# A graph network's last 96 nodes updated in three sets of 32 across the partitions' quarters, and the last messages' mish in three parts

## The chip, the cores and the metric

The kernel runs on one core of a Trainium2 chip. The metric is the device time of one execution in microseconds (us); the time of a version is the median of its runs. Engines are called TensorE (PE in the profile), VectorE (DVE), ScalarE (ACT), GpSimd (POOL) and SyncE (SP, which here only issues DMAs).

## The reference

625 nodes with 512 features and 20,000 edges sorted by their target pass through four graph layers, each behind a layer norm, a relu and a residual. The change touches only the fourth. In it, per edge and then per node:

```
def mish(x):
    return x * jnp.tanh(jax.nn.softplus(x))
edge_feat = jnp.concatenate([x[src], x[dst], edge_attr], axis=-1)
h = mish(edge_feat @ W1 + b1)
messages = mish(h @ W2 + b2)
agg = jax.ops.segment_sum(messages, dst, num_segments=x.shape[0])
u = mish(jnp.concatenate([x, agg], axis=-1) @ W3 + b3)
out = u @ W4 + b4
y = x + out
return (y - mu) * jax.lax.rsqrt(var + LN_EPS) * gamma + beta
```

## The kernel before

The fourth layer is `layer3_near`. Edges come in 160 tiles of 125, four to a group, 40 groups (NG = 40, g = 0 to 39). A hand-written loop over steps s = 0 to 44 is a software pipeline: in step s group s gets its first product, group s-2 its second, group s-4 is summed into its targets, and group s-5's sums are added to the nodes' sums. The stages are:

- `rows` (two steps ahead): edge features by SP, gathered node rows by POOL.
- `first(g)`: TensorE makes z for 500 edges (L1327, L1332), DVE adds the bias (L1334) and writes a copy bounded at 20 (`bounded`, L1291). `quotients` then lets ACT compute the factor of the mish in place, exp (L1299), ln(1 + .) (L1301), tanh (L1303), and DVE multiplies it in (L1477). Exp then ln then tanh need two loads of ACT's function tables; `set_of_exp` (L1307) loads the table that holds exp and ln ahead of need.
- `second(g)`: four tiles of 16 products, each evicted by DVE with its bias (L1348) to the messages; one step later they are bounded into `um`, go through ACT, and in the step after that are multiplied (L1468). The last group has parts of its own: its messages are bounded in two halves (tiles 0-1 and 2-3) as soon as they are there, ACT does exp and ln of each half and then both tanh (L1490 to L1493), and `sent` multiplies by halves (L1361).
- `sent(g)`: TensorE sums messages to a window of 32 nodes through a one-hot (L1370), with the 512 features in four quarters of the partitions; DVE copies the sum (L1374).
- `collected(g)`: a transpose (L1380), and DVE adds it into mT, the nodes' sums (L1381).

The nodes are updated in five sets of 125 (c = 0 to 4), each when the last group that reaches into it has been collected: `last_of` is 8, 16, 24, 32 and 39. With last group L, `update_u` (products with W3, L1391; add, L1394; bounded copy, L1291) is in step L+5, ACT's three functions in L+6, `update_mul` (L1399) and `update_turn` (four transposes, L1405; copy to uT, L1407) in L+7, `update_out` (products with W4, L1422; add, L1424; statistics, L1425, L1426) in L+8, and `update_root`, `update_end` (square root on ACT, L1431; normalization, L1435 to L1441; store, L1443) in L+9. Set 4 has no steps left: its whole chain, and the root and end of set 3, stand behind the loop. Set 4's output is made in two halves of 256 columns.

What sets the order: everything wrapped in `keep` stays in program order on its engine, so DVE and ACT work through the loop body as written, in order. TensorE's instructions are placed by the scheduler, and are also executed in the order that it gives. A tile from a pool takes one of `bufs` buffers of its tag. Whoever writes a buffer anew waits until the last reader of the tile before it is done. PSUM tiles of `ps` have six buffers. The node updates use tags with one buffer each:

```
u = lp.tile([128, D], F32, tag="u", name="u", bufs=1)[:P]
us["u", c] = bounded(u, P, D, "uu", 1)
uT = lp.tile([128, D], F32, tag="uu", name="uT", bufs=1)[:, :KD * P]
```

So the bounded copy of a set and the transposed u of a set share the one buffer `uu`.

Of the kernel before, what the change touches and what calls it, by code (L numbers as in the profile page):

```python
# [9 lines left out]
F32 = mybir.dt.float32  # L10
F16 = mybir.dt.float16
I32 = mybir.dt.int32
AF = mybir.ActivationFunctionType
# [181 lines left out]
def gnn_body(ctx: ExitStack, tc: tile.TileContext, a: dict, out: bass.AP, consts, near: bool):  # L195
# [1028 lines left out]
    def layer3_near(wts, wm2, own, h_tabs, uh):  # L1224

        keep = tc.keep_in_program_order
        with tc.tile_pool(name="layer3n", bufs=2) as lp, banks("c", 6):
# [65 lines left out]

            width = {"uz": G * D}

            def quotients(v):

                for u in v:
                    keep(nc.scalar.activation(u, u, AF.Exp))  # L1299
                for u in v:  # L1300
                    keep(nc.scalar.activation(u, u, AF.Ln, bias=1.0))  # L1301
                for u in v:
                    keep(nc.scalar.activation(u, u, AF.Tanh))  # L1303
# [34 lines left out]
            def second(g):  # L1338

                z = zs.pop(g)  # L1340
                w = G // z.shape[1]
                m = lp.tile([P, G, D], F32, tag="mess", name="mess", bufs=3)
                for j in range(G):
                    p = ps("z2")
                    for f in range(KD):
                        nc.tensor.matmul(p[:P, :], z[:, j // w, f, j % w * P:(j % w + 1) * P], wm2[:, f, :],  # L1346
                                         start=f == 0, stop=f == KD - 1)
                    keep(nc.vector.tensor_add(m[:, j, :], p[:P, :], bc["b2"]))  # L1348
                    if g == NG - 1 and j % 2:

                        us["m", g, j // 2] = bounded(flat(m[:, j - 1:j + 1, :]), P, 2 * D, "uz", 2)
                ms[g] = m

            def sent(g):


                m = ms.pop(g)
                if g == NG - 1:
                    for n in range(2):
                        v = flat(m[:, 2 * n:2 * n + 2, :])  # L1360
                        keep(nc.vector.tensor_mul(v, v, us.pop(("m", g, n))))  # L1361
                base = base_of(g)
                acc[g] = pools["acc"].tile([128, 128], F32, tag="acc", name="agg3", bufs=2)
                o = work.tile([P, G, W], F32, tag="oh", name="oh")
                nc.vector.tensor_tensor(o, iota_f[:, None, base:base + W].to_broadcast([P, G, W]),
                                        dst_f[:, g * G:(g + 1) * G, None].to_broadcast([P, G, W]),
                                        op=ALU.is_equal)
                for j in range(G):
                    for i in range(KD):
                        nc.tensor.matmul(acc[g][i * W:(i + 1) * W, :], o[:, j, :],  # L1370
                                         m[:, j, i * 128:(i + 1) * 128], start=j == 0, stop=j == G - 1,
                                         skip_group_check=True, tile_position=(0, i * W))
                v = lp.tile([128, 128], F32, tag="ag", name="ag", bufs=2)
                keep(nc.vector.tensor_copy(v, acc[g]))  # L1374
                acc[g] = v
# [7 lines left out]
                                          mT[:, :, base:base + W]))  # L1383


            last_of = [max(g for g in range(NG) if base_of(g) < (c + 1) * P) for c in range(NC)]

            def update_u(c):
                p = ps("u")
                for k in range(KD):  # L1390
                    nc.tensor.matmul(p[:P, :], mT[:, k, c * P:(c + 1) * P], late["w"][:, k, :],  # L1391
                                     start=k == 0, stop=k == KD - 1)
                u = lp.tile([128, D], F32, tag="u", name="u", bufs=1)[:P]
                keep(nc.vector.tensor_add(u, p[:P, :], uh[:, c, :]))  # L1394
                nodes[c] = u
                us["u", c] = bounded(u, P, D, "uu", 1)

            def update_mul(c):
                keep(nc.vector.tensor_mul(nodes[c], nodes[c], us.pop(("u", c))))  # L1399

            def update_turn(c):
                u = nodes.pop(c)
                t = ps("tr")
                for k in range(KD):
                    nc.tensor.transpose(t[:, k * P:(k + 1) * P], u[:, k * 128:(k + 1) * 128], ident[:P, :P])  # L1405
                uT = lp.tile([128, D], F32, tag="uu", name="uT", bufs=1)[:, :KD * P]
                keep(nc.vector.tensor_copy(uT, t[:, :KD * P]))  # L1407
                nodes[c] = uT

            def update_out(c):  # L1410
                uT = nodes.pop(c)
                y = h[:, c, :]

                n = 2 if c == NC - 1 else 1
                stats = work.tile([P, 2, 6], F32, tag="stats3", name="stats3", bufs=NC)[:, :n]
                mv = work.tile([P, 2], F32, tag="mv1", name="mv1", bufs=NC)
                rstd = work.tile([P, 1], F32, tag="rstd1", name="rstd1", bufs=NC)
                for i in range(n):
                    cols = slice(i * D // n, (i + 1) * D // n)
                    p = ps("o3")  # L1420
                    for k in range(KD):
                        nc.tensor.matmul(p[:P, :D // n], uT[:, k * P:(k + 1) * P], late["wm4"][:, k, cols],  # L1422
                                         start=k == 0, stop=k == KD - 1)
                    keep(nc.vector.tensor_add(y[:, cols], p[:P, :D // n], y[:, cols]))  # L1424
                    keep(nc.vector.bn_stats(stats[:, i, :], y[:, cols]))  # L1425
                keep(nc.vector.bn_aggr(mv, stats))  # L1426
                nodes[c] = y, mv, rstd

            def update_root(c):
                y, mv, rstd = nodes[c]  # L1430
                keep(nc.scalar.activation(rstd, mv[:, 1:2], AF.Sqrt, bias=eps))  # L1431

            def update_end(c):
                y, mv, rstd = nodes.pop(c)
                keep(nc.vector.reciprocal(rstd, rstd))  # L1435
                n = 2 if c == NC - 1 else 1
                for i in range(n):
                    cols = slice(i * D // n, (i + 1) * D // n)
                    keep(nc.vector.scalar_tensor_tensor(y[:, cols], y[:, cols], mv[:, 0:1], bc["gamma"][:, cols],
                                                        op0=ALU.subtract, op1=ALU.mult))  # L1440
                    keep(nc.vector.scalar_tensor_tensor(x[:, c, cols], y[:, cols], rstd, x[:, c, cols],  # L1441
                                                        op0=ALU.mult, op1=ALU.add))
                    (nc.scalar if i else nc.sync).dma_start(out[c * P:(c + 1) * P, cols], x[:, c, cols])  # L1443

            def biases(c):
                keep(nc.vector.tensor_add(uh[:, c, :], uh[:, c, :], bc["b3"]))
# [5 lines left out]
            for s in range(NG + 5):  # L1452
# [8 lines left out]
                if s == 0:  # L1461
                    for n in range(2):
                        quotients([us["z", 0, n]])
                        z = flat(zs[0][:, n])
                        keep(nc.vector.tensor_mul(z, z, us.pop(("z", 0, n))))  # L1465
                if s - 4 in ms and s - 4 < NG - 1:
                    m = flat(ms[s - 4])
                    keep(nc.vector.tensor_mul(m, m, us.pop(("m", s - 4))))  # L1468
                if s - 3 in ms and s - 3 < NG - 1:
                    us["m", s - 3] = bounded(flat(ms[s - 3]), P, G * D, "um", 1)  # L1470
                quotients([us[k] for k in (("z", s, 0), ("m", s - 3), *(("u", c) for c in range(NC - 1) if s - 6 == last_of[c])) if k in us])
                for c in range(NC - 2):
                    if s - 9 == last_of[c]:
                        update_root(c)
                if s - 1 in zs and s > 1:
                    z = flat(zs[s - 1][:, 0])
                    keep(nc.vector.tensor_mul(z, z, us.pop(("z", s - 1, 0))))  # L1477
                for c in range(NC - 1):
                    if s - 7 == last_of[c]:
                        update_mul(c)  # L1480
                if s == 1:
# [2 lines left out]
                if 1 <= s - 2 < NG:  # L1484
                    second(s - 2)
                if s - 2 == NG - 1:
                    v = [us["m", NG - 1, n] for n in range(2)]
                    set_of_exp()
                    for u in v:
                        keep(nc.scalar.activation(u, u, AF.Exp))  # L1490
# [1 line left out]
                    for u in v:  # L1492
                        keep(nc.scalar.activation(u, u, AF.Tanh))  # L1493
                    set_of_exp()
                for c in range(NC - 1):
                    if s - 7 == last_of[c]:
                        update_turn(c)
                    if s - 8 == last_of[c]:
# [2 lines left out]
                        update_end(c)  # L1501
                if 9 <= s < 9 + NC:
                    biases(s - 9)
                if 0 <= s - 4 < NG:
                    sent(s - 4)
                if 0 <= s - 5:
                    collected(s - 5)
                for c in range(NC - 1):
                    if s - 5 == last_of[c]:
                        update_u(c)  # L1510
            c = NC - 1
            update_u(c)
            quotients([us["u", c]])
            update_root(c - 1)
            update_mul(c)
            update_turn(c)
            update_end(c - 1)
            update_out(c)
            update_root(c)
            update_end(c)  # L1520

    if near:
        wts2 = ctx.enter_context(tc.tile_pool(name="wts2", bufs=1))
# [87 lines left out]
```

## Time and profile before

| what | value |
|---|---|
| median of 7 runs | 1801.81 us (1798.13 to 1806.59) |
| profiled execution's own time | 1799.09 us |
| its span, first to last instruction | 1797.3 us |
| PE, DVE, ACT, POOL busy | 94%, 56%, 42%, 45% of the span |
| TensorE's mean granted clock | 0.977 of full speed |
| largest line | L1346 (`second`), 556.2 us of PE |

The page counts an engine busy while it executes; an idle time is put down to the instruction whose end released the next one. Late in the kernel a step of the loop takes some 18.7 us (two starts of L1346, 1690.68 and 1709.42). Times below are us from the start of the span.

### The profile page before, as it was taken

How to read it: one execution, taken by the hardware profiler on the slowest of the kernel's cores; microseconds unless marked ns; L12 is line 12 of the kernel's file. 1: busy time of each engine (PE TensorE's matmuls, PEld its weight loads, DVE VectorE, ACT ScalarE, POOL GpSimd, SP SyncE). 2: the span in 40 equal slices, each digit the busy share in tenths (PEclk: the TensorE clock that was granted, in tenths of full speed). 3: DMA queues.
4: the chain of work that ended last, by engine and by line, in shares of the span. 5: the costliest groups of instructions: out<-in, count | busy, mean ns of one | idle time of the engine just before them, and what ended most of it. 6: DMA issues, size and time to landing. Idle time of an engine off the chain costs nothing.

```text
span 1797.3 us, 24375 instructions
## 1 busy us (share of the span) xinstructions
PE 1696.8 (94%) x9770; PEld 876.6 (49%) x9770; DVE 1013.3 (56%) x1697; ACT 761.4 (42%) x792; POOL 811.9 (45%) x479
## 2 busy tenths in 40 slices
PE   4878999999999889999999899999999999999995
PEld 4878544444444334444544444445444444544443
DVE  7997210002000478877854667777666776667663
ACT  2452110000000312222214676766686687668664
POOL 0000000000000377665715888888887788788300
PEclk9999999999999989999999999999999999999996
DMA  2001030020000296756535587666666666667300
GB/s 74 3 3 51 4 133 14 0 94 6 0 0 0 65 203 162 173 153 165 145 88 142 105 175 150 128 117 117 122 127 108 123 129 118 111 115 135 46 1 14
DMA packets 157219, 162.59 MB, mean 90 GB/s; under 512 B 97546, under 2 KB 104059, under 8 KB 157096
## 3 DMA queue, kind: packets, MB, share of 16 engines
q0 software_dynamic: 131584, 119.48, 34.1%
q1 hardware_dynamic: 20100, 32.69, 5.8%
q10 hardware_dynamic: 5412, 8.77, 1.7%
q8 instruction: 79, 1.29, 0.3%
q14 instruction: 44, 0.36, 0.1%
HBM read 155.11 MB, written 5.12 MB: 89 GB/s over the span
## 4 chain that ended last, share of the span: by engine, by line
PE 86%; DVE 4%; issue 3%; DMA 3%; ACT 2%; POOL 1%; DVEq 0%; ACTq 0%; POOLq 0%; SPq 0%
PE z L1346 29%; PE agg L661 10%; PE hb L648 8%; PE sum L961 6%; PE tpw L938 4%; PE q L538 4%; PE z L1332 4%; PE z L1327 4%; PE agg L1370 2%; PE xsd L1040 2%; PE agg L637 2%; PE l L613 2%; PE mlp L890 2%; PE nsum L606 1%; PE u L1391 1%
## 5 line engine op out<-in xcount | busy, mean ns | idle before, releaser
L1346 PE MATMUL z<-wm,z 128*125 128x512 f32 x1280 | 556.2, 592 | 2.7 <-DVE z L1465 2.7
L1346 PEld LDWEIGHTS z<-wm,z 128*125 128x125 f32 x1280 | 237.2, 188 | 293.1 <-issue 269.9
L281 POOL DMA_INDIRECT g_s<-xs,src_i x160 | 296.3, 1852 | 124.2 <-issue 75.7
L281 POOL DMA_INDIRECT g_s<-xd,dst_i x144 | 307.4, 2135 | 43.9 <-issue 42.6
L902 POOL MEMSET mT<- 128x5000 f32 x1 | 4.3, 4265 | 585.8 <-PE tr L843 585.8
L281 POOL DMA_INDIRECT gup<-up,src_i x160 | 199.5, 1247 | 107.2 <-issue 39.7
L1348 DVE TENSOR_TENSOR mess<-z,b 125x512 f32<-125x512 f32 x160 | 106.3, 686 | 134.8 <-PE z L1346 134.8
L661 PE MATMUL agg<-hb,adj 125*125 125x512 f32 x400 | 173.6, 592 | 0.0
L651 DVE COPY hb<-hb 125x512 f32<-125x512 f32 x20 | 13.8, 692 | 263.0 <-PE hb L648 263.0
L945 DVE TENSOR_TENSOR msg<-tpw,gup 125x768 f32<-125x768 f32 x160 | 151.4, 946 | 0.0
L538 PE MATMUL q<-rh,ohs 125*128 125x96 bf16 (+1 forms) x2400 | 120.4, 213 | 28.4 <-DVE ohs L556 26.3
L1334 DVE TENSOR_SCALAR z<-z,b 128x500 f32<-128x500 f32 (+1 forms) x164 | 108.4, 718 | 59.3 <-PE z L1332 57.5
L1299 ACT ACTIVATE uz<-uz 128x2000 f32<-128x2000 f32 (+1 forms) x41 | 75.0, 1829 | 151.3 <-DVE uz L1291 151.3
L648 PE MATMUL hb<-basis,hT 128*125 128x512 f32 x320 | 138.6, 592 | 0.0
L538 PEld LDWEIGHTS <-ohs 125*128 125x128 bf16 x2400 | 115.3, 101 | 33.7 <-DVE ohs L556 32.9
L961 PE MATMUL sum<-msg,ohy 125*32 125x256 f32 (+2 forms) x1600 | 125.8, 392 | 0.0
L653 ACT COPY hb<-hb 125x512 f32<-125x512 f32 x20 | 11.7, 586 | 260.1 <-PE hb L648 240.2
L661 PEld LDWEIGHTS agg<-hb,adj 125*125 125x125 f32 x400 | 74.8, 188 | 94.7 <-issue 94.7
L961 PEld LDWEIGHTS sum<-msg,ohy 125*32 125x32 f32 x1600 | 74.8, 110 | 85.7 <-issue 60.3
L938 PE MATMUL tpw<-w,hid 64*125 64x512 f32 x320 | 99.3, 649 | 6.4 <-DVE msg L945 6.4
L1299 ACT ACTIVATE um<-um 125x2048 f32<-125x2048 f32 x39 | 74.5, 1910 | 71.1 <-DVE um L1291 71.1
L943 DVE TENSOR_TENSOR msg<-tpw,gup 125x256 f32<-125x256 f32 x160 | 66.6, 416 | 59.4 <-PE tpw L938 29.3
(210 smaller groups left out, 2207.4 us busy)
## 6 DMA issues: line engine op xcount, KB each, us to landing
rt<-in_edge_attr SPq DMA_DIRECT2D x76, 125.0 KB
basis<-in_L_gnn_basis SPq DMA_DIRECT2D x8, 1024.0 KB
gup<-up,src_i POOLq DMA_INDIRECT x160
g_s<-xs,src_i POOLq DMA_INDIRECT x160
g_s<-xd,dst_i POOLq DMA_INDIRECT x144
w<-in_L_gnn_W SPq DMA_DIRECT2D x2, 1024.0 KB
loop<-in_L_gnn_loop SPq DMA_DIRECT2D x2, 1024.0 KB
w1ab<-in_L_gnn_W ACTq DMA_DIRECT2D x1, 2048.0 KB
```

The lines of the kernel that those rows point to most:

```text
L281: return nc.gpsimd.indirect_dma_start(out=dst, out_offset=None, in_=table, in_offset=bass.IndirectOffsetOnAxis(ap=idx[:, t:t + 1], axis=0) ...
L538: nc.tensor.matmul(q[c][:, :n, o:o + WT], hot[j][:, c, :], rhs[j][:, q0:q0 + n, :], start=j + k == 0, stop=j == GS - 1 and k == 2, skip_gr ...
L648: nc.tensor.matmul(p[:P, :], hT[:, k, s * P:(s + 1) * P], basis[b][:, k, :], start=k == 0, stop=k == KD - 1)
L661: nc.tensor.matmul(acc[c], adj[:, s - 1, l * NB + b, c * P:(c + 1) * P], hb[:, b, :], start=False, stop=s == NC and b == NB - 1)
L938: nc.tensor.matmul(p[:P, :], hid[s // 2][s % 2][rws, i * P:(i + 1) * P], w4[rws].rearrange("p k u -> p (k u)"), start=True, stop=True)
L945: nc.vector.tensor_mul(m[:, :, 1:, :], pv[:, 2:4, None, :].to_broadcast([P, 2, 3, MUL]), g[:, None, 1:, :].to_broadcast([P, 2, 3, MUL]))
L961: nc.tensor.matmul(A[r * W:(r + 1) * W, cs, :], oh[:, j, q, :], v, start=j % G == 0 and r not in done, stop=j % G == G - 1, skip_group_che ...
L1299: keep(nc.scalar.activation(u, u, AF.Exp))
L1327: nc.tensor.matmul(pf[f][:, :ne], w[half, f * 128:(f + 1) * 128], rt[half, cols], start=True, stop=False)
L1334: keep(nc.vector.tensor_scalar(zv[:, n, f, :], pf[f][:, :ne], b1[:, f:f + 1], None, op0=ALU.add))
L1346: nc.tensor.matmul(p[:P, :], z[:, j // w, f, j % w * P:(j % w + 1) * P], wm2[:, f, :], start=f == 0, stop=f == KD - 1)
L1348: keep(nc.vector.tensor_add(m[:, j, :], p[:P, :], bc["b2"]))
```

## The change

Set 4 is cut in two. Its first 29 rows (nodes 500 to 528) stay a set 4 and go through the loop like sets 0 to 3: their last group is 34, so `update_u(4)` falls into step 39, `update_mul(4)` and `update_turn(4)` into 41, `update_out(4)` into 42. The other 96 nodes (529 to 624) are updated in three sets of 32 with last groups 36, 38 and 39: `late_u(j)` makes their product with W3 with the four quarters of the features in the four quarters of the partitions, in steps 41, 43 and 44, into one tile of 128 x 384. Behind the loop that tile goes through one mish, three transposes and one copy, and then through the output in two halves as set 4 did. The roots and ends of set 3 and of the 29 rows stand there too. `late_rows` moves the rows of h, x and uh that belong to the 96 nodes to other partitions, by DMAs on SP in steps 14 to 17.

The last messages (group 39) are bounded, put through ACT and multiplied in three parts, tiles 0-1, 2 and 3. Group 38's bounded copy goes into a buffer of `uz`, ahead of group 37's multiplication, with the table of exp and ln loaded ahead of it.

```diff
+            ends = ((0, 1), (2,), (3,))
+            ND = 96
+            first_d = N - ND
+            def rows_of(c):
+                return P if c < NC - 1 else P - ND
...
+                    for n, js in enumerate(ends):
+                        if g == NG - 1 and j == js[-1]:
+                            if n == 0:
+                                us["last"] = lp.tile([128, G * D], F32, tag="uz", name="uz", bufs=2)[:P]
+                            us["m", g, n] = us["last"][:, js[0] * D:(j + 1) * D]
+                            keep(nc.vector.tensor_scalar_min(us["m", g, n], flat(m[:, js[0]:j + 1, :]), 20.0))
...
             def update_u(c):
+                n = rows_of(c)
...
-                us["u", c] = bounded(u, P, D, "uu", 1)
+                us["u", c] = bounded(u, n, D, "uu", 1)
...
+            def late_rows(i):
+                c, r0 = NC - 1, P - ND
+                if i == 0:
+                    late_nodes["y"] = late["w"][:ND, KD, :]
+                    late_nodes["x"] = late["w"][:ND, KD + 1, :]
+                    late_nodes["u"] = late["b"][:, 0, :ND * KD]
+                    keep(nc.sync.dma_start(late_nodes["y"], h[r0:, c, :]))
+                    keep(nc.sync.dma_start(late_nodes["x"], x[r0:, c, :]))
+                else:
+                    j = i - 1
+                    for r in range(KD):
+                        keep(nc.sync.dma_start(late_nodes["u"][r * W:(r + 1) * W, j * 128:(j + 1) * 128],
+                                               uh[r0 + j * W:r0 + (j + 1) * W, c, r * 128:(r + 1) * 128]))
+            def late_u(j):
+                p = ps("u")
+                at = first_d + j * W
+                for k in range(KD):
+                    for r in range(KD):
+                        nc.tensor.matmul(p[r * W:(r + 1) * W, :128], mT[:, k, at:at + W],
+                                         late["w"][:, k, r * 128:(r + 1) * 128], start=k == 0, stop=k == KD - 1,
+                                         skip_group_check=True, tile_position=(0, r * W))
+                u = late_nodes["u"][:, j * 128:(j + 1) * 128]
+                keep(nc.vector.tensor_add(u, p[:, :128], u))
+            def late_turn():
+                u = late_nodes["u"]
+                t = ps("tr")
+                for j in range(ND // W):
+                    nc.tensor.transpose(t[:, j * 128:(j + 1) * 128], u[:, j * 128:(j + 1) * 128], ident)
+                uT = lp.tile([128, D], F32, tag="u", name="uT", bufs=1)[:, :KD * ND]
+                keep(nc.vector.tensor_copy(uT.rearrange("p (k j n) -> p j k n", k=KD, n=W),
+                                           t[:, :KD * ND].rearrange("p (j k n) -> p j k n", k=KD, n=W)))
+                return uT
...
+                if s - 3 == NG - 2:
+                    set_of_exp()
+                    us["m", s - 3] = bounded(flat(ms[s - 3]), P, G * D, "uz", 2)
                 if s - 4 in ms and s - 4 < NG - 1:
                     m = flat(ms[s - 4])
                     keep(nc.vector.tensor_mul(m, m, us.pop(("m", s - 4))))
-                if s - 3 in ms and s - 3 < NG - 1:
+                if s - 3 in ms and s - 3 < NG - 2:
                     us["m", s - 3] = bounded(flat(ms[s - 3]), P, G * D, "um", 1)
-                quotients([us[k] for k in (("z", s, 0), ("m", s - 3), *(("u", c) for c in range(NC - 1) if s - 6 == last_of[c])) if k in us])
+                quotients([us[k] for k in (("z", s, 0), ("m", s - 3), *(("u", c) for c in range(NC) if s - 6 == last_of[c])) if k in us])
...
+                if 0 <= s - 9 - NC <= ND // W:
+                    late_rows(s - 9 - NC)
                 if 0 <= s - 4 < NG:
                     sent(s - 4)
                 if 0 <= s - 5:
                     collected(s - 5)
-                for c in range(NC - 1):
+                for c in range(NC):
                     if s - 5 == last_of[c]:
                         update_u(c)
-            c = NC - 1
-            update_u(c)
-            quotients([us["u", c]])
-            update_root(c - 1)
-            update_mul(c)
-            update_turn(c)
-            update_end(c - 1)
-            update_out(c)
-            update_root(c)
-            update_end(c)
+                for j in range(ND // W):
+                    if s - 5 == last_of_d[j]:
+                        late_u(j)
+            u = late_nodes["u"]
+            us["u"] = bounded(u, 128, KD * ND, "uu", 1)
+            quotients([us["u"]])
+            for c in (NC - 2, NC - 1):
+                update_root(c)
+            keep(nc.vector.tensor_mul(u, u, us.pop("u")))
+            uT = late_turn()
+            for c in (NC - 2, NC - 1):
+                update_end(c)
+            normed(NC, uT, late_nodes["y"], ND, 2)
+            update_root(NC)
+            update_end(NC)
```

`normed` is the body of the old `update_out` with the rows and the number of halves as arguments; `update_out(c)` calls it with one half.

## The prediction

> **What bounds the kernel now.** I first read the page's shares: TensorE is busy for 94% of the span. The chain of waits from 1700 us on then shows where this ends. Its columns are start, length, engine and line; "x" counts records, two per fp32 product.
>
> ```profile
> 1725.02 13.73 PE z L1346 x32
> 1738.75 3.45 PE o L1422 x8
> 1742.22 0.70 DVE h L1424
> ...
> 1744.10 2.20 DVE mess L1468
> ...
> 1747.73 1.91 ACT um L1299
> ...
> 1768.77 6.27 PE u L1391 x8
> 1775.07 0.70 DVE u L1394
> ...
> 1782.19 6.39 PE o L1422 x16
> ```
>
> Until 1742 TensorE sets the time: whatever is added there in steps 39 and 40 is paid. Then DVE and ACT carry the mish of groups 38 and 39, and after 1768.77 set 4's update runs by itself. TensorE's last second product (group 39) ends at 1757.23, beside that chain.
>
> The timeline gives prices and the DVE order around step 39.
>
> ```profile
> 1683.41 3.70 PE L1391 MATMUL u<-wm3b,aT 128*125 128x512 f32 x8 [0.39 <-DVE aT L1381]
> 1687.15 0.69 DVE L1394 TENSOR_TENSOR u<-u,uh 125x512 f32<-125x512 f32 x1 [3.59 <-PE u L1391]
> 1687.87 0.43 DVE L1291 TENSOR_SCALAR uu<-u 125x512 f32<-125x512 f32 x1
> ...
> 1727.71 2.29 DVE L1468 TENSOR_TENSOR mess<-mess,um 125x2048 f32<-125x2048 f32 x1 [2.17 <-ACT um L1303]
> 1730.04 1.23 DVE L1291 TENSOR_SCALAR um<-mess 125x2048 f32<-125x2048 f32 x1
> 1731.18 2.23 DVE L1477 TENSOR_TENSOR z<-z,uz 128x2000 f32<-128x2000 f32 x1
> ...
> 1765.35 2.12 PE L1370 MATMUL agg<-mess,oh 125*32 125x128 f32 x32 [1.21 <-DVE mess L1361]
> ```
>
> The first row is set 3's product with W3 inside the loop: 3.70 us, against 6.26 behind it. The table by stretches says why (last columns: granted clock, DMA share, GB/s).
>
> ```profile
> 1756.00:1758.00 2.00, 2.00 (x35) 1.00 (x33) 0.74 (x2) 1.97 (x3) 0.00 (x0) 1.00 0.00 0
> 1760.00:1762.00 2.00, 0.70 (x16) 0.66 (x20) 1.45 (x2) 1.95 (x3) 0.00 (x0) 0.58 0.00 0
> 1772.00:1774.00 2.00, 2.00 (x3) 0.66 (x2) 0.00 (x0) 0.00 (x0) 0.00 (x0) 0.51 0.00 0
> 1774.00:1776.00 2.00, 1.03 (x3) 0.19 (x1) 0.90 (x2) 0.00 (x0) 0.00 (x0) 1.00 0.00 0
> ```
>
> After some 2 us with little work the clock halves, and it is back 5.2 us after the products resume at 1768.77.
>
> **What the change removes behind the loop.** (a) Product with W3: 6.26 us becomes one `late_u` of 32 records of 128 columns. That is the form of L1370: 1.08 us at full clock (row at 1757.12), 2.12 at half. I take 1.9, since the clock before it was low: -4.4. (b) The rest up to the output (add 0.69 to 0.29 as L1381; bounded copy, three functions, multiplication and copy at 384 instead of 512 columns, by the 512 and 1024 column rows -0.07, -0.36, -0.13, -0.13; three transposes of four, -0.27): -1.37. The output keeps its 16 records of 256 columns (6.4). The two ends beside it take 2 x 1.6 = 3.2 us of DVE from uT on, under the 3.8 us until the first half is there: 0 (0.15 + 0.73 + 0.75 each; all of 1.6 more if TensorE ran at full clock there).
>
> **What it adds to the loop.** (c) Step 39: the 29 rows' product. Rows don't shorten it, the columns are again 512. Set 3's insertion: next product at 1687.04, 4.34 after its transpose at 1682.70, where otherwise 0.17 lies between (1724.69 to 1724.86): **+4.17** on TensorE, on the path. (d) Step 42: output of the 29 rows, 3.45 us of TensorE, and add, statistics, aggregate on DVE; DVE works in order, so group 39's multiplications stand behind them. (e) Step 43: `late_u(1)` stands on TensorE between group 39's sums and their transpose. Before, 1.30 us pass from the end of the sums to the next product (1767.47 to 1768.77). After: 0.65 until group 38's sums are in mT, 1.08 to 2.12 (I take 1.6) for `late_u(1)`, 0.86 for transpose and add: 3.1, **+1.8**. (f) ACT in step 40: three functions of 512 columns, 3 x 0.62. (g) `late_rows`: 14 DMAs on SP, ahead of edge features that are loaded two steps, some 37 us, before use: 0; exposed they'd cost SP's 0.27 us per issue, 3.8 in all. Nothing on SP goes away, so no gain.
>
> **The wait it adds.** Tag `uu` has one buffer. Set 3's uT is in it from step 39 until its output products in step 40 have read it. Before, the next bounded copy comes behind the loop. Now the 29 rows' bounded copy is at the end of step 39, in DVE's order ahead of group 36's multiplication; in the changed program it waits for the last of set 3's output products on TensorE. TensorE does not wait for DVE until then, so it runs through group 38's second product and that output, and DVE stands still. No row shows this wait; its bounds are 0 (if DVE's queue had slack) and the whole stretch from 1729.8 to 1746.4, 16.6 us. I follow the queue:
>
> - The copy is ready at 1725.40 + 3.63 + 0.8 = 1729.8 and goes when the output is done, 1742.22 + 4.17 = 1746.4.
> - Behind it: group 36's multiplication to 1749.2, group 37's bounded copy to 1750.3, z of group 39 to 1752.5 (steps of the rows above: 0.45, 2.33, 1.14, 2.16).
> - TensorE idles: group 36's sums need that multiplication (1749.2), and group 39's second product the z and a PSUM buffer that DVE empties next: start 1753.2 instead of 1743.30. At 13.9 us it ends at 1767.1.
> - Between 1746.4 and 1753.2 TensorE has 1.4 us of work, so the clock halves as at 1760. Cost of that between 0 and 6.95 (all 13.9 us of full-clock work run at half speed would be 27.8, but the 5.2 us row says it returns); 5.2 us at half speed lose 2.6. I take that: end E = 1769.7.
> - ACT: group 37's bounded copy is there at 1750.5 instead of 1731.36. Three functions of 1.91, three of 0.62, two tables of 1.28: 1760.7. Table 1762.0; group 38 without its first table load: 7.0, 1769.0. Table 1770.3; the last messages' exp and ln, 2.06 + 1.25 + 1.25 = 1774.9; table 1.28, first tanh done 1777.2 (before: 1763.9).
> - DVE: from E the add and bounded copy of tile 3 (1.15), small copies, `late_u(0)` (1.1), its add, then the 29 rows' output (3.47 from E+3.2) and 1.8 for add, statistics and aggregate: group 39's multiplications start at E+8.5 = 1778.2, later than ACT. Three of 1.2, 0.65, 0.65: 1780.7; the last tile's sums 0.3 to 0.5: 1781.1, where before 1767.47.
>
> **The sum.** Sums end +13.6; (e) +1.8; (a) and (b) -5.8. Together **+9.6** in the profiled execution, 1799.09 to 1808.7. The median lies 2.7 above that execution, so 1811.4; I say 1811.
>
> The change's own gain in ACT (group 38's bounded copy 2.3 earlier, one table load of 1.28 less, a short last part) is in these numbers: it is real, but starts 19 us late.
>
> [...]
>
> **The rivals.**
>
> *The wait costs nothing* (TensorE bound throughout, DVE catches up). For it: DVE is busy only 56% of the span. Against: DVE's work of groups 36 to 38 stands behind it, 16 us of stall against a step of 18.7. Then E = 1757.23 + 4.17 = 1761.4, multiplications at E+8.5 = 1769.9, sums done 1772.7, +5.2; with +1.8 and -5.8 +1.2: 1803.0, no change.
>
> *Faster: the moved work hides.* The place is TensorE in steps 39 to 42: if it had 4.2 us to spare there and the 29 rows' output left DVE's queue free, the last group's mish would decide. E stays 1757.23, exp of tile 3 at E+1.25, three tanh done at E+6.1, sums done 1765.0 instead of 1767.47: -2.5; with (a) and (b) -5.8, `late_u(1)` hidden: -8.3, 1793.5. It decides from the point where TensorE's idle time before 1742 exceeds 4.2 us. For it: DVE and ACT carry the chain from 1742 on. Against: the chain is TensorE without a gap before that.
>
> *The clock stays down* through the 29 rows' output and both `late_u` too: 3.5 + 1.0 more, minus what ACT covers: up to +13.5, 1815.3. This is the forecast's upper end.
>
> **How the numbers follow.** A measurement here tells no change from about 0.2%, 3.6 us. Forecast (with its clock variants) 0.85, wait for nothing 0.10, faster 0.05. The forecast's own range is +7.3 (full clock all along, then ACT decides) to +13.5. Half of the "wait costs nothing" case is to be in the range as well, and its upper half with one cold `late_u` reaches 1804.5; so 1804.5 to 1815.5. Slower by over 0.2%: 0.87; within: 0.08; faster: 0.05.
>
> **What would show it.** In the changed kernel's trace: the bounded copy of 29 x 512 in `uu` starting when set 3's output (o, 128x512) ends, some 16 us after its add, and listed as the longest of DVE's late waits, with TensorE as releaser; TensorE idle for some 6 us between the output of set 3 and group 39's second product, and a granted clock near 0.5 behind it; ACT idle from step 39 to group 37's exp; `late_u` of 1 to 2 us each, and the stretch from the last `late_u` to the output 1.4 us shorter than 7.2. I am wrong if that copy starts within 1 us of its add; then it is the second case.

## The result, and the profile after

| | before | after |
|---|---|---|
| median, lowest to highest | 1801.55 us (46 runs, 1795.14 to 1809.67) | 1809.85 us (19 runs, 1805.15 to 1815.09) |
| ratio to before, 95% interval | 1 | 1.0044 [1.0033, 1.0055] |
| profiled execution, its span | 1799.09, 1797.3 us | 1807.5, 1805.7 us |
| tail, as defined below | 91.45 us | 98.43 us |

The change costs 8.3 us by the medians. Runs of one kernel differ by up to 17 us, and among the traces below the tail begins anywhere from 1702.68 to 1726.84, so much of the difference arises ahead of it. To compare single executions I therefore use the **tail**: from the start of group 39's first product (L1327 before, L1336 after) to the end of the span. It begins at 1705.85 before and 1707.27 after, so every time of the changed kernel below stands 1.42 us later than the same event of before. The tail is 6.98 us longer, which is most of the 8.3.

The chain of waits of the changed kernel, columns as in the prediction, tells the story from top to bottom (L1433 is set 3's output, then the 29 rows', and last that of the 96):

```profile
1726.82 3.62 PE u L1405 x8
1730.44 13.93 PE z L1355 x32
1744.37 3.45 PE o L1433 x8
1747.84 0.41 DVE uu L1291
1748.26 2.21 DVE mess L1528
1750.49 1.23 DVE um L1291
1751.72 2.15 DVE z L1537
1753.87 0.61 DVE mess L1357
1754.52 15.74 PE z L1355 x32
...
1773.35 2.98 PE o L1433 x7
...
1778.65 2.35 DVE mess L1373 x3
...
1784.81 2.01 PE u L1465 x32
...
1792.73 5.12 PE o L1433 x16
```

First the 29 rows' product (L1405), group 38's second product and set 3's output, all on TensorE. Then five pieces of DVE in a row, 6.6 us, with none of TensorE: before, the chain had no such stretch until 1742. The piece that the wait releases is the first, `uu` at L1291. The timeline (start, length, engine, line, operation; in brackets the idle time before it and what ended it) shows how long DVE stood:

```profile
1730.48 0.68 DVE L1408 TENSOR_TENSOR u<-u,uh 29x512 f32<-29x512 f32 x1 [3.51 <-PE u L1405]
1747.84 0.41 DVE L1291 TENSOR_SCALAR uu<-u 29x512 f32<-29x512 f32 x1 [16.68 <-PE o L1433]
...
1751.81 1.91 ACT L1308 ACTIVATE um<-um 125x2048 f32<-125x2048 f32 x1 [22.71 <-DVE um L1291]
...
1777.24 2.10 ACT L1553 ACTIVATE uz<-uz 125x1024 f32<-125x1024 f32 x3
1778.58 2.41 DVE L1373 TENSOR_TENSOR mess<-mess,uz 125x1024 f32<-125x1024 f32 x3
```

The add at 1730.48 has left its result ready at 1731.2; the 0.41 us copy behind it runs at 1747.84, when set 3's output (o, L1433) has ended. ACT has meanwhile been idle for 22.71 us, because its next input (group 37's `um`) is queued on DVE behind that copy. The waits of DVE from 1650 us on (waiter, releaser, total, times, longest) put it in one row:

```profile
DVE mess L1357 <- PE z L1355: 16.9, 10, 2.7
DVE uu L1291 <- PE o L1433: 16.7, 1, 16.7
```

Ten ordinary waits for the second products add up to what this single wait takes. The stretches (window, length, then busy time and count for PE, PEld, DVE, ACT and POOL; last columns granted clock, DMA share, GB/s) show the clock after it:

```profile
1748.00:1750.00 2.00, 0.00 (x0) 0.00 (x0) 2.00 (x2) 0.00 (x0) 0.00 (x0) 1.00 0.00 0
1750.00:1752.00 2.00, 1.29 (x32) 0.84 (x32) 1.97 (x3) 0.19 (x1) 0.00 (x0) 0.81 0.00 0
...
1756.00:1758.00 2.00, 2.00 (x3) 0.66 (x2) 2.00 (x7) 1.98 (x3) 0.00 (x0) 0.50 0.00 0
1758.00:1760.00 2.00, 2.00 (x6) 0.94 (x5) 1.25 (x2) 1.99 (x2) 0.00 (x0) 0.98 0.00 0
```

In the first idle stretch the full clock is still granted. It halves at about 1751.2 (0.81 over the second row), and is back at about 1758, 3.5 us after the products of group 39 began. That is why `second` of group 39 takes 15.74 us and not 13.9.

### The profile page after: what moved, and what is told of

It reads as the page before. It is cut to its first block, busy times and chain, and to the rows that moved or that the text cites. A ratio compares the mean times of both kernels' runs of the same rounds, so it can differ in the third digit from the quotient of the medians.

```text
span 1805.7 us, 24636 instructions
## 1 busy us (share of the span) xinstructions
PE 1707.5 (95%) x9877; PEld 881.4 (49%) x9877; DVE 1016.0 (56%) x1711; ACT 763.4 (42%) x799; POOL 813.0 (45%) x479
## 3 DMA queue, kind: packets, MB, share of 16 engines
HBM read 155.11 MB, written 5.12 MB: 89 GB/s over the span
## 4 chain that ended last, share of the span: by engine, by line
PE 87%; issue 4%; DVE 4%; DMA 3%; ACT 1%; POOL 0%; DVEq 0%; POOLq 0%; ACTq 0%; SPq 0%
PE z L1355 30%; PE agg L661 10%; PE hb L648 8%; PE sum L961 6%; PE z L1336 4%; PE tpw L938 4%; PE q L538 4%; PE z L1341 4%; PE agg L1382 2%; PE xsd L1040 2%; PE agg L637 2%; PE l L613 2%; PE mlp L890 2%; PE nsum L606 1%; DMA gup<-up,src_i 1%
## 5 line engine op out<-in xcount | busy, mean ns | idle before, releaser
L1308 ACT ACTIVATE uz<-uz 128x2000 f32<-128x2000 f32 (+2 forms) x42 | 76.9, 1831 | 154.7 <-DVE uz L1291 154.7
```

## The experiments

Two theories. **W**, the prediction's: the shared buffer `uu` makes DVE wait, and this wait is the loss. **Q**, the rival: the wait is covered, and the loss is the added work itself (29 rows' product and output, `late_u`) in TensorE's and DVE's queues. The first four kernels ran on one chip (before: 1798.39 us, 29 runs), the last four on another, slower one (before: 1814.9, 17 runs), so they are compared by the ratio to before on the same chip; it is estimated from the single runs and is not exactly the quotient of the two medians. Tails are of one execution each. The last column is where group 39's sums end, counted from the start of the tail: 61.69 us before, 74.25 in the changed kernel. Behind that point stands the last output, which takes between 5.1 and 6.7 us in these traces, in before and the changed kernel by where the clock returns (last section), so differences of tails below some 1.6 us show nothing by themselves.

| kernel | median us | ratio to before, 95% | tail us | last sums end, us |
|---|---|---|---|---|
| e1, own buffer | 1800.66 | 1.0004 [0.9987, 1.0021] | 92.04 | 66.79 |
| e2, mish part alone | 1798.42 | 1.0003 [0.9989, 1.0017] | 89.67 | 60.29 |
| e3, sets alone | 1808.98 | 1.0054 [1.0036, 1.0072] | 102.37 | 77.40 |
| e6, four sets of 32 | 1797.19 | 0.9989 [0.9975, 1.0002] | 89.62 | 63.25 |
| e10, longer read of the buffer | 1828.46 | 1.0081 [1.0059, 1.0102] | 102.43 | 78.08 |
| e8, clock kept up | 1825.2 | 1.0070 [1.0043, 1.0096] | 98.26 | 74.40 |
| e9, 29 rows one step later | 1825.91 | 1.0080 [1.0050, 1.0109] | 97.46 | 72.11 |
| e7, e6 reordered | 1811.93 | 0.9978 [0.9958, 0.9999] | 83.46 | 60.88 |

On the second chip the medians lie 2.6 to 5.0 us higher against before than the tails do, with 12 runs of e7 and four or five of the others, and neither before's trace nor a run of the changed kernel was taken there. The medians don't tell e8, e9 and e10 apart; what is said of these three rests on one trace each.

### e1: the 29 rows get a buffer of their own

```
-                us["u", c] = bounded(u, n, D, "uu", 1)
+                us["u", c] = bounded(u, n, D, "uu" if c < NC - 1 else "uv", 1)
```

> The changed kernel, but the 29 rows' bounded copy has a buffer of its own instead of the shared uu. Theory W (the wait for that one buffer makes the loss): DVE's stall of 16.7 us ends, group 39's second product starts without a gap and without a halved clock, and the time falls by some 8 us against the changed kernel, to about 1802 to 1804 (ratio to before 1.000 to 1.0015): what stays is +4.2 for the 29 rows' product, DVE's queue in step 42 and late_u(1), against -5.8 at the end. Theory Q (the added work itself makes the loss: TensorE's product and output of the 29 rows, and DVE's part of that output ahead of group 39's multiplications; the stall is covered): the time stays within 2 us of the changed kernel, 1808 to 1811, ratio 1.004.

The loss is gone: 1.0004, and a tail 6.39 us shorter than the changed kernel's, 0.59 longer than before's. The last sums end 7.46 us earlier than in the changed kernel; 1.38 of that are lost again in the last output (6.50 us against 5.12). W holds and Q does not. Its chain of waits around the place:

```profile
1728.22 3.62 PE u L1405 x8
1731.84 13.93 PE z L1355 x32
1745.76 3.43 PE o L1433 x8
...
1750.47 13.73 PE z L1355 x32
...
1767.29 2.94 PE o L1433 x7
...
1772.59 2.35 DVE mess L1373 x3
```

No DVE piece lies between set 3's output and group 39's second product, which takes 13.73 us, as group 38's does before (1725.02, granted clock 1.00), and ends at 1764.20. What then holds group 39's multiplications until 1772.5 is the 29 rows' output in DVE's queue: the first tanh of group 39's messages was done at about 1769.1.

### e10: the buffer is read for 3.4 us longer

Set 3's output product is made a second time, into a PSUM tile that nothing reads.

```
...
+                if c == NC - 2:
+                    p = ps("again")
+                    for k in range(KD):
+                        nc.tensor.matmul(p[:n, :], uT[:, k * n:(k + 1) * n], late["wm4"][:, k, :],
+                                         start=k == 0, stop=k == KD - 1)
```

> The changed kernel, and set 3's output products are made a second time into a PSUM tile that nobody reads (wasted work, 3.45 us of TensorE, in a stretch where TensorE is idle for 6.7 us anyway). The transposed u of set 3 is so held 3.45 us longer. Measure: the tail, from the start of group 39's first product to the end of the span (before 91.45, changed kernel 98.43). W: the wait of the 29 rows' bounded copy grows from 16.7 to some 20.1 us and all that follows shifts: tail about 101.9, time about 3.4 us above the changed kernel's 1809.85. Q (the stall is covered): the second output is in idle time, tail 98 to 99.

The timeline of this kernel:

```profile
1758.87 0.41 DVE L1291 TENSOR_SCALAR uu<-u 29x512 f32<-29x512 f32 x1 [20.12 <-PE again L1447]
1762.84 1.91 ACT L1308 ACTIVATE um<-um 125x2048 f32<-125x2048 f32 x1 [26.14 <-DVE um L1291]
```

The copy's wait grows from 16.68 to 20.12 and ACT's from 22.71 to 26.14, 3.4 us each, and the releaser is now the last reader added. The last sums end 3.83 us later (the tail grows by 4.00): 3.44 of the longer wait, and 0.40 of `second` of group 39, which takes 16.14 here instead of 15.74. A wait that is lengthened by 3.4 and paid with 3.8 is on the path in full.

### e8: the clock is kept up through the stall

`filler(n)` puts n products of weights into an unread PSUM tile: three behind set 3's output, three at group 36's sums.

```
+            def filler(n):
+                p = ps("fill")
+                for _ in range(n):
+                    nc.tensor.matmul(p[:P, :], wm2[:, 0, :P], wm2[:, 1, :], start=True, stop=True)
...
```

> The changed kernel with six products of 512 columns on weights (wasted, 0.86 us each) behind set 3's output and around group 36's sums, in the 6.7 us in which TensorE is idle, so that the clock does not halve. Group 39's second product then takes 13.9 us instead of 15.7. If TensorE's end of it sets the time of group 39's multiplications: tail 1.8 us shorter than 98.4, 96.6. If ACT does (its first tanh of the last messages ended 0.3 us before DVE began to multiply): tail 98.1, the halved clock cost next to nothing.

`second` of group 39 takes 13.90 us here, 1768.87 to 1782.77, near the 13.93 of group 38's in the changed kernel (granted clock 1.00), and ends 1.66 us earlier in the tail. But the tail is 98.26, 0.17 below the changed kernel's, and the last sums end 0.15 later: keeping the clock gains nothing. The chain of waits says what decides instead:

```profile
1762.01 0.41 DVE uu L1291
...
1764.65 1.24 DVE um L1291
1765.98 1.91 ACT um L1308
...
1777.20 1.92 ACT uz L1308
...
1791.41 1.06 ACT uz L1560
1792.50 1.24 DVE mess L1373
```

From the wait on, the chain runs through ACT without a gap to the last messages' tanh: the mish of groups 37, 38 and 39 and of the 29 rows in a row, 26.5 us, started late by the wait. So the stall costs by two chains of nearly equal length, TensorE with the halved clock and ACT; taking the clock's loss away leaves ACT.

### e9: the 29 rows one step later, buffer still shared

```
+            step_of = last_of[:NC - 1] + [last_of[NC - 1] + 1]
```

and `step_of` in place of `last_of` in the seven conditions of the loop that place a set's update.

> The changed kernel, uu still one buffer, but the 29 rows' set runs one step later (product in step 40 behind set 3's output, functions in 41 with group 38's, multiplication and transposes in 42, output in 43). W: the bounded copy no longer finds uu held, DVE's stall is gone without a second buffer; ACT gets three functions of 0.62 in its critical step and the output stands on TensorE in step 43 ahead of the last sums, so the tail is 93 to 96 instead of 98.4, ratio to before 1.001 to 1.0025. Q: as much work on the path as in the changed kernel or more, 98 or above.

The stall is gone from the timeline:

```profile
1761.44 0.68 DVE L1409 TENSOR_TENSOR u<-u,uh 29x512 f32<-29x512 f32 x1 [2.75 <-PE u L1406]
1762.15 0.41 DVE L1291 TENSOR_SCALAR uu<-u 29x512 f32<-29x512 f32 x1
```

The copy follows its add by 0.03 us. But the tail is 97.46, 0.97 below the changed kernel's, where W had wanted 2.4 us or more. Part of that is the last output, 6.41 us here: the last sums end 2.14 earlier, against 7.46 in e1. The chain shows the price that replaces the wait:

```profile
1783.30 4.58 PE o L1434 x8
1787.90 0.69 DVE h L1436
...
1789.50 2.32 DVE mess L1373 x3
```

`second` of group 39 ends as early as in e1 (55.1 us into the tail, there 55.5). The 29 rows' output now stands in step 43 and takes 4.58 us instead of 3.45, by which an estimated 2.3 us of it, twice the difference, are at half clock, and group 39's multiplications wait for its add and statistics in DVE's order: they start 69.3 us into the tail, 63.9 in e1. W's tail of 93 to 96 was a miss, Q's 98 or above too, and the median (1.0080) shows no gain over the changed kernel at all; what Q says of DVE's queue is real in this place. e9 moves more than the wait, so it does not speak against e1 and e10.

### e2 and e3: the two halves of the change

e2 is the kernel before with the messages' mish in three parts and group 38's bounded copy ahead; e3 is the changed kernel without them.

```
-            ends = ((0, 1), (2,), (3,))
+            ends = ((0, 1), (2, 3))
...
-                if s - 3 == NG - 2:
-                    set_of_exp()
-                    us["m", s - 3] = bounded(flat(ms[s - 3]), P, G * D, "uz", 2)
```

> The kernel before with the second half of the change alone: last messages' mish in three parts, group 38's bounded copy ahead of group 37's multiplication with the table loaded ahead. Set 4 stays whole behind the loop. W and Q alike expect a small gain, since neither the wait nor the 29 rows are there: ACT ends group 38 some 3.7 us earlier, then TensorE's end of the second product decides, sums done about 2.5 us earlier: 1799, ratio 0.9986. If three parts cost more than they save (one more exp, ln, tanh and multiplication with their fixed parts), 1802 or more.

> The changed kernel without the mish part: the last messages in halves again, group 38's bounded copy in um behind group 37's multiplication, no table ahead of it. W: the stall pushes group 37's functions on ACT late, so ACT's order then decides and the missing table load and parts cost: 2 us above the changed kernel, 1811 to 1813, ratio 1.0055. Q: the mish part only matters where ACT decides; if TensorE and DVE do, it is the same as the changed kernel, 1809 to 1810.

e2's tail is 1.78 us shorter than before's, its last sums end 1.40 earlier; the whole time, known to 0.14%, can't show that (1.0003 where 0.9986 was expected). e3's tail is 3.94 longer than the changed kernel's, its last sums end 3.15 later. In these traces the mish part is worth more where ACT is late: e3's chain of waits,

```profile
1745.10 0.41 DVE uu L1291
...
1751.79 16.46 PE z L1355 x32
...
1776.01 1.28 ACT L1547
1777.30 1.07 ACT uz L1547
1778.39 2.37 DVE mess L1370 x2
```

goes through ACT's table load and tanh into the multiplications, behind the same `uu`. So the loss comes with the sets, and the mish part lessens it. In the traces both signs are as W had them. For the size of e3, W's 2 us is some 1 us too small by the last sums; its ratio of 1.0054 is the one that W expected, but the interval also holds Q's 1.0044.

### e6 and e7: without the set of 29, then reordered

e6 cuts the last 128 nodes (497 to 624) into four sets of 32 and leaves set 3 with 122 rows, so that no small set goes through the loop and nothing but set 3 uses `uu` in it.

```
-            ND = 96
+            ND = 128
...
-                return P if c < NC - 1 else P - ND
+                return P if c < NC - 2 else (N - ND) - c * P
```

> The changed kernel with all of the last 128 nodes in four sets of 32 in the quarters (late_u four times), set 3 cut to 122 rows, and no set of 29 rows: no second user of uu in the loop, no 29-row product, no 29-row output. Late tile 128 x 512. W and Q both expect a gain here, W because the wait is gone, Q because the work is gone: late_u(0) costs 1.1 to 1.6 on TensorE in step 39, sums done about 1 us before those of the kernel before, late_u instead of the whole product -4.3, the add -0.4, late_u ahead of the last transpose +1.8: about 1797 to 1798, ratio 0.9975.

1797.19, 3.5 us under e1 on the same chip, and a tail 1.83 below before's; the ratio of 0.9989 [0.9975, 1.0002] is not clear of no change. The last sums end 1.56 us later than before's, where some 1 us earlier was expected; the gain comes behind them. Group 39's multiplications start here at 1762.59, though the first tanh is done at 1760.55, and one `late_u` (at 1766.49, 1.94 us) stands between the last sums and their transpose, with another behind it:

```profile
1762.67 1.14 DVE mess L1374
...
1769.22 1.41 PE u L1470 x32
```

e7 takes both away by order alone: group 38's multiplication goes ahead of the eviction of group 39's last tile, and the collection of group 38 with its `late_u` goes ahead of group 39's sums.

```
+                    if g == NG - 1 and j == G - 1:
+                        v = flat(ms[g - 1])
+                        keep(nc.vector.tensor_mul(v, v, us.pop(("m", g - 1))))
...
+                if s - 4 == NG - 1:
+                    collected(s - 5)
+                    late_u(2)
+                    sent(s - 4)
+                    late_add(2)
+                    continue
```

> The four sets of 32 (no set of 29 rows), and three moves: group 38's multiplication ahead of tile 3's eviction in the second product of group 39, where DVE is idle for 2.3 us; group 38's collection and late_u of the third set ahead of group 39's sums; that set's add behind them. Expected from the trace of the four sets: group 39's multiplications start when ACT's first tanh is done, 2.0 us earlier, and 2.7 us between the last sums and the last late_u go down to 1.3 (no late_u between): tail 89.6 - 3.5 = about 86, time about 1793 to 1794, ratio 0.997.

```profile
1782.36 1.28 ACT L1565
1783.65 1.06 ACT uz L1565
1784.74 2.44 DVE mess L1377 x3
...
1788.81 1.13 PE u L1473 x32
```

In its chain ACT's last table load and tanh decide when the multiplications start (1784.74 follows 1784.71), and one `late_u` is left behind the sums, of 1.13 us (L1370's form takes 1.08 before at a granted 1.00). The tail is 83.46, 8.0 below before's and some 2.5 below what was expected. The median is 0.9978 [0.9958, 0.9999]: faster than before, by 0.0 to 0.4%. The interval ends at 7.6 us, so the median does not confirm the whole 8.0 of the tail.

## Why the prediction was right, and where a size was off

The sign and the cause were right, and the size nearly so: 1811 forecast, 1809.85 measured, +9.6 against +8.3 by the medians and +6.98 in the tail. That the medians come so near is in part luck: of the 8.4 us between the two profiled executions 1.42 lie ahead of the tail, where the prediction has no term. Its sum, term by term, with the measured tail split at the same points (after's times less 1.42):

| term | forecast | measured | from |
|---|---|---|---|
| last sums end later | +13.6 | +12.56 | 1781.52 against 1767.54 |
| `late_u(1)` between sums and next product | +1.8 | +2.06 | 3.29 us against 1.23 |
| last product with W3 until the output | -5.8 | -5.50 | 7.92 against 13.42 |
| last output | 0 | -1.27 | 5.12 against 6.39 |
| from the output to the end of the span | 0 | -0.87 | 7.85 against 8.72 |
| sum | +9.6 | +6.98 | |

- **The wait** is as forecast: 16.68 us against 16.6, released by set 3's output, the longest single late wait of DVE, and caused by the shared buffer (e1 takes it away by a second buffer and nothing else; e10 lengthens it and the time follows).
- **(c), the 29 rows' product**, is on TensorE's path as forecast: in the changed kernel's chain, 1724.74 to 1730.44 holds the transpose, sums, DVE's two pieces and the product with no other work between them. Set 3's output ends 4.20 us later in the tail than before (1747.82 against 1742.20), where +4.17 was forecast.
- **Mis-sized: the halved clock.** Forecast 2.6 us of loss; 15.74 less 13.9 is 1.84. This accounts for 0.76 of the 1.04 us by which the sums came earlier than forecast. e8 shows further that this term was not a term by itself: at that point ACT was level with TensorE, the first tanh ending at about 1778.3 and DVE free at 1778.58. The prediction had them 1 us apart and added the clock's loss in full.
- **`late_u`**: taken as 1.6 and 1.9, measured 1.93 and 2.01, near the second price of L1370's two (1.08 and 2.12) in both places: the granted clock is 0.50 from 1782 on.
- **Not foreseen: the last output.** I had kept its 6.4 us. It is 5.12 here, 6.50 in e1, 5.85 in e7 and 6.70 in e6, for the same 16 records of 256 columns; between here and before the granted clock differs: it returns about 2.9 us after the output's start here and 5.4 in before. Half of that first part and all of the rest make 3.7 us of full-clock work in both; with these 3.7 the lengths give an estimated 5.6 in e1, 4.3 in e7 and 6.0 in e6. I take this -1.27 for luck and not for an effect of the change; one trace of each kernel does not show which it is. The last row, -0.87, is nearly all behind the last DVE instruction, where only the store of 96 rows instead of 125 is left; that the rows are the reason is only argued.
- **The rival "the wait costs nothing"** gave +1.2, with group 39's second product ending at 1761.4 and the multiplications from 1769.9. e1 is that case, made: in before's times 1761.39 and 1769.71, and +0.59 in the tail. Its last sums end 5.10 us later than before's, for which this rival had 5.2. Steps (a) to (f), without the wait, were thus right to within a microsecond in their sum, and the wait's own share of the last sums was 7.46 us (74.25 less 66.79), forecast as 8.4 (13.6 less 5.2).
- **(g), the 14 DMAs**, cost nothing, as forecast, though SP took some 15.0 us over issuing them (0.59 us for each of the first two, 2.68, 6.09 and 5.01 for the three times four) where I had put 3.8: my 0.27 us is what SP took for a store of the output, the cheapest issue in before's trace, whose edge loads take from 0.47 to 3.35. Across these steps the loop of e1, which has them, keeps before's pace: eleven steps of edge loads take 219.92 us there (from 1194.12) and 220.72 before (from 1189.71). In the changed kernel's trace the first of these steps is 1.7 us longer; since e1 has the same DMAs without that, they do not bring it about by themselves, and what does stays open. It is more than the 1.42 us by which the tail begins later.
- **The rival "faster"** fails where the prediction said: TensorE has no 4.2 us to spare before set 3's output, which ends 4.20 later. e6 and e7 show that the update can go into the loop without a loss once the 29 rows are not in that place. That e7's tail, -8.0, lies near the -8.3 of this rival is chance: e7 has reorderings that the rival has not.

What stays open: why the medians give 1.3 us more than the tails here, and 2.6 to 5.0 more for the four kernels on the second chip. The executions differ by more than that upstream, and one tail of each kernel can't settle it.

## What to carry to other kernels

When work is put into a loop earlier than its neighbours, look up each buffer that it takes anew and who reads that buffer last: with one buffer per tag and an engine that works in order, the wait stops everything behind it, here for 16.7 us with DVE busy only 56% of the span. A second buffer of 2 KB per partition was worth 6.4 us of the tail; the same step put one place later removed the wait too, but gave most of it back in the queue (e9). Where two chains end level, pricing one of them alone (the clock here) overstates what it costs. And where single executions are compared, choose a point ahead of work whose time hangs on the clock: here the end of the last sums shows 2.14 us of e9's gain, the tail 0.97.

## What the runs showed of the hardware

- As the prediction had it, 29 rows cost TensorE as much as 125 here: 3.62 us for the product with W3 against set 3's 3.70 before, and in the output 3.36 us for the 29 rows' two pieces in the changed kernel's chain, 3.45 for set 3's.
- The granted clock near the end of before's trace, in stretches of 1 us, columns as above:

```profile
1758.00:1759.00 1.00, 0.56 (x10) 0.24 (x2) 1.00 (x4) 0.97 (x2) 0.00 (x0) 1.00 0.00 0
1759.00:1760.00 1.00, 0.23 (x1) 0.04 (x1) 1.00 (x2) 1.00 (x2) 0.00 (x0) 1.00 0.00 0
1760.00:1761.00 1.00, 0.00 (x0) 0.00 (x0) 1.00 (x1) 0.97 (x2) 0.00 (x0) 0.65 0.00 0
...
1777.00:1778.00 1.00, 0.00 (x0) 0.00 (x0) 0.00 (x0) 0.98 (x2) 0.00 (x0) 0.68 0.00 0
...
1787.00:1788.00 1.00, 1.00 (x5) 0.80 (x4) 0.00 (x0) 0.00 (x0) 0.00 (x0) 0.70 0.02 8
```

TensorE is fully busy until about 1758.5, partly until 1759.2, then idle; at about 1760.3, 1.1 us later, the granted clock halves (0.65 over the third row). In that trace it is back at about 1774.0, halves again at 1777.4 and is back at 1787.6, 5.4 us after the start of the last output, which takes 6.39 us. In the changed kernel it is back at about 1795.6, 2.9 us after the start of that output, which takes 5.12; the longest is e6's with 6.70. What sets the times of these changes was not shown.
